# Attention and involution in one kernel: the first block's queries ahead of the last keys, and the last image's products and weights asked for at other points

## The chip, the cores and the metric

The kernel runs on one core of a Trainium2 chip. The metric is the device time of one execution in microseconds (us). Before the change it is 2611.5 us, the median of three runs (2610.78 to 2611.92).

## The reference

The input x is 4 images of 512 channels and 64 x 64 pixels, in float32. Two layers follow each other:

```
# layer 0: attention over all 4096 pixels of an image
q, k, v = wq x + bq, wk x + bk, wv x + bv          # 128 channels each
attn = softmax(q^T k)
x = wo (v attn^T) + bo + x
# layer 1: involution, 7 x 7, in 8 groups of 16 channels
o1 = relu(W1 x * s1 + b1)                          # 128 channels
w  = Ws relu(Wr o1 * sr + br) + bs                 # 49 taps x 8 groups, for every pixel
out[g, c] = sum over taps of w[g, tap] * o1[g, c] shifted by the tap
x = W3 out * s3 + b3 + x
```

## The kernel before, in words

**Tiles and order.** Pixels are cut into 8 chunks of 512 (8 rows of the image). For each image the kernel first makes all keys and values (`keys_values`, line 438), in the order of `KEYS`: chunks 2 to 7, then 1, then 0. For a chunk that is 4 matmuls into `pk`, an activation on ScalarE that writes the keys, 16 matmuls of 128 columns into `pv`, and a copy on ScalarE that writes the values. Then `attention` (line 609) goes through the chunks again as blocks of queries: in each block 32 steps of one score matmul (`pss`), an exp on ScalarE (`pt`), one matmul with the values (`po`) and one add of `pt` on VectorE (`pacc`). Scores are issued two steps ahead of `po`. The queries of a block (`queries`, line 472: 4 matmuls into `pq` and an activation) are made eight steps before the block begins. Only the first block of an image has them made at the head of `attention` (line 617), after the last values. In the last image the last block is split in two halves of 256 pixels (blocks 7 and 8).

**What runs beside attention.** Each finished block is taken over by `finish_block` (line 482), a generator that divides by the softmax sum (`sums`, `blocks`, `pl`, `rls`, `spread`, `on`), projects back (`pwo`), adds the input, makes o1 (`p1`), writes it pixel by pixel to DRAM (`pix`), and makes the reduced channels from which the tap weights follow (`pr`, `red`). The involution (`involution`, line 301) works in units of 4 image rows, 16 in an image. For a unit TensorE makes the tap weights of all its pixels (`weights`, line 270, into the PSUM tile `pw`); VectorE multiplies windows of o1, read back from DRAM into the SBUF tile `ring`, by the weights (`prod`, or `acc` for the first, line 351), 14 to 21 products a unit; and GpSimd adds the products up (line 375). `prod` has 4 buffers. TensorE then turns the sum (`turn_unit`, line 390), and `close_chunk` (line 419) projects it (`py`), adds it to x and stores.

**Who sets the order.** The order is written by the program itself with an account of time. `mm` (line 213) adds each matmul's reckoned time to `pe`, and `takes` adds each operation of another engine to `free[...]`. After every attention step `chores` (line 264) runs one step of the list `finishing`, one of `closing`, and then `pace` (line 227), which offers products as far as they are due and as the account lets VectorE and GpSimd take them (VectorE's queue up to 4.5 us ahead in the last image, 3.5 in the others). A generator that waits for a point of the account uses `until`; in the involution line 308 waits until VectorE will be free, plus 0.3 us, before a unit's weights are made:

```python
            yield from until(free["dve"] + 0.3)
            pw = early.pop((b, u), None) or weights(b, u)
```

A scheduler may then shift instructions that don't depend on each other. While attention runs, `pw` has one PSUM buffer; a second is opened once it is over (line 682).

**The tail.** When the last block's steps are out, `tail` is set. From there nothing waits for the account, every second product is added on TensorE by matmuls with the identity (`pa`) in place of GpSimd, and the rest of `finishing`, `closing` and the units is written out in turns until all is stored.

Of the kernel before, what the change touches and what calls it, by code (L numbers as in the profile page):

```python
# [13 lines left out]
B, C, H, W = 4, 512, 64, 64  # L14
# [3 lines left out]
CH = 512  # L18
# [52 lines left out]
HOP_US = 0.8  # L71
STEP_US = 1.0
POOL_LAG = 4.0, 7.5
PIECE = 3
TB = 32
WARM = 8
# [7 lines left out]
def fast_path(  # L84
# [68 lines left out]
    pe = 0.0  # L153
    due, seen = 0.0, 0.0
    free = {"dve": 0.0, "pool": 0.0, "dma": 0.0}
    tail = []
    reds, sums_c = {}, {}
    written = {}
# [4 lines left out]
    def until(us):  # L163
        while pe < us and not tail:
            yield "wait"
# [9 lines left out]
    def load_x(b, c):  # L175
        xs[b, c] = xpool.tile([P, CT, CH], F32, tag="x", name=f"x_{b}_{c}")
        takes("dma", X_US)
        nc.sync.dma_start(xs[b, c], x_r[b, :, :, c * CH : (c + 1) * CH])
# [38 lines left out]
    def step(queue, n):  # L217
        while n and queue:
            try:
                if next(queue[0]) in ("wait", "none"):  # L220
                    return False
                n -= 1
            except StopIteration:
                queue.pop(0)
        return not n
# [36 lines left out]
                load = (b + 1) * STEP  # L262

    def chores():
        step(finishing, 1)
        step(closing, 1)
        pace()
# [33 lines left out]
    def involution():  # L301
        nonlocal low, due
        while True:
            while not units:
                yield "none"
            b, u = units.pop(0)
            acc = work2.tile([P, NT, 4, P], F32, tag="acc", name=f"acc_{b}_{u}")
            yield from until(free["dve"] + 0.3)
            pw = early.pop((b, u), None) or weights(b, u)
            begin = pe + 0.5  # L310
            pa, ops = None, []
            base = b * STEP + u * UR
            for dy0, n in DYS:

                at = (base + dy0) % RING
                whole = at + n + NT < RING + 1
                pieces = [(dy0, n)] if whole else [(dy0, 2), (dy0 + 2, n - 2)]
                ops += [(x, dy, k) for x in range(K) for dy, k in pieces]
            for o, (x, dy, n) in enumerate(ops):
                if o and dy >= DYS[1][0] > ops[o - 1][1]:  # L320
                    low = base + UR
                    pump()
                    if tail and units:
                        early[units[0]] = weights(*units[0])
                rows = [(base + dy + t * 2) % RING for t in range(NT)]
                while base + dy + n + NT > load:
                    yield "wait"
                landed = max(landing[base + dy + i] for i in range(n + NT))
                while not tail and (
                    pe < max(begin, landed)  # L330
                    or free["dve"] > pe + (4.5 if b == B - 1 else 3.5)
                    or free["pool"] > pe + lag
                ):
                    yield "wait"
                free["pool"] = max(free["pool"], takes("dve", DVE_TAPS[0] + DVE_TAPS[1] * n))
                takes("pool", POOL_TAPS[0] + POOL_TAPS[1] * n)
                due -= n
                d0 = dy - DYS[dy >= DYS[1][0]][0]
                first = x == 0 and dy < DYS[1][0]
                prod, p0 = acc, d0  # L340
                if not first:
                    prod, p0 = prods.tile(
                        [P, NT, 4, P], F32, tag="prod", name=f"prod_{b}_{u}_{o}"
                    ), 0
                col = (x * K + dy) * G
                lines = ring[:, rows[0] : rows[0] + n, x, :]
                image = bass.AP(
                    tensor=lines.tensor, offset=lines.offset,
                    ap=[lines.ap[0], [(rows[1] - rows[0]) * K * P, NT], [K * P, n], [1, P]],
                )  # L350
                product = nc.vector.tensor_tensor(  # L351
                    prod[:, :, p0 : p0 + n, :].rearrange("p t d (g c) -> p t d g c", g=G),
                    image.rearrange("p t d (g c) -> p t d g c", g=G),
                    pw[:, :, col : col + n * G].unsqueeze(3)
                    .broadcast_to([P, NT, n * G, GC])
                    .rearrange("p t (d g) c -> p t d g c", d=n),
                    ALU.mult,
                )
                if lag == POOL_LAG[0]:
                    tc.keep_in_program_order(product)  # L360
                if first:
                    pass
                elif tail and o % 2:

                    begun = pa is not None
                    if not begun:
                        pa = ps1.tile([P, NT, P], F32, tag=("po", "acc")[u % 2], name=f"pa_{b}_{u}")
                    for t in range(NT):
                        for d in range(n):
                            mm(  # L370
                                pa[:, t, :], prod[:, t, d, :], ident,
                                not begun and t == d == 0, False,
                            )
                else:
                    nc.gpsimd.tensor_tensor(  # L375
                        acc[:, :, d0 : d0 + n, :], acc[:, :, d0 : d0 + n, :], prod[:, :, :n, :],
                        ALU.add,
                    )
                yield
            low = max(low, (b + 1) * STEP if u == NU - 1 else base + UR)  # L380
            pump()
            if pa is None:
                for n in (2, 1):
                    nc.gpsimd.tensor_tensor(  # L384
                        acc[:, :, :n, :], acc[:, :, :n, :], acc[:, :, n : 2 * n, :], ALU.add
                    )
            closing.append(turn_unit(b, u, acc, pa, takes("pool", POOL_OP * 1.5)))
# [50 lines left out]
    def keys_values(b):  # L438
        kt = kvpool.tile([P, N], F32, tag="k", name=f"k_{b}")
        vT = kvpool.tile([P, N // P, P], F32, tag="v", name=f"v_{b}")  # L440

        for i, c in enumerate(KEYS):
            for k in KEYS[i + 1 : i + 3]:
                if (b, k) not in xs:
                    load_x(b, k)
            if b < 2 and i == 4:
                for rows in (slice(0, PAD), slice(PAD + H, None)):
                    nc.sync.dma_start(pix[b][rows].rearrange("r w c -> w r c"), zero)
                for cols in (slice(0, PAD), slice(PAD + W, None)):
                    nc.sync.dma_start(pix[b][PAD : PAD + H, cols, :], zero[:H])  # L450
            xt = xs[b, c] if c < KEEP else xs.pop((b, c))
            pk = ps_s.tile([P, CH], F32, tag="s", name=f"pk_{b}_{c}")
            for t in range(CT):
                mm(pk, w_slice(O_WK, t), xt[:, t, :], t == 0, t == CT - 1)
                if t % 2:
                    chores()
            nc.scalar.activation(
                kt[:, c * CH : (c + 1) * CH], pk, AF.Identity, bias=v1(V_BK)
            )
            pv = ps1.tile([P, 4, P], F32, tag=("po", "acc")[i % 2], name=f"pv_{b}_{c}")  # L460
            for j in range(4):
                for t in range(CT):
                    mm(
                        pv[:, j, :], xt[:, t, j * P : (j + 1) * P], w_slice(O_WV, t),
                        t == 0, t == CT - 1,
                    )
                if j % 2:
                    chores()
            nc.scalar.copy(vT[:, 4 * c : 4 * c + 4, :], pv)
        return kt, vT  # L470

    def queries(b, c, off, n):
        xt = xs[b, c][:, :, off : off + n]
# [132 lines left out]
            yield from tell()  # L606


    def attention(b, kt, vT):
        blocks = [(c, 0, CH) for c in range(NCH)]  # L610
        if b == B - 1:

# [1 line left out]

        steps = [(k, j) for k, (_, _, n) in enumerate(blocks) for j in range(N // P * n // CH)]
        qs, pts, pos, paccs = {}, {}, {}, {}
        qs[0] = queries(b, *blocks[0])

        def score(m):
            k, j = steps[m]  # L620
# [47 lines left out]
    for b in range(B):  # L668
        lag = POOL_LAG[0]
        kv = keys_values(b)  # L670
        lag = POOL_LAG[1]
        if b == 0:

            pb = ps.tile([P, CT], F32, tag="mm", name="pb")
            for t in range(CT):
                tc.keep_in_program_order(mm(pb[:, t : t + 1], w_slice(O_WO, t), v1(V_BVC)))
            bo = const.tile([P, CT], F32, name="bo")
            nc.vector.tensor_tensor(bo, pb, vec[:, V_BO : V_BO + CT], ALU.add)
        attention(b, *kv)
    tail.append(True)  # L680
    scorepool.close()
# [405 lines left out]
```

## Time and profile before

| | us |
|---|---|
| median of the runs | 2611.5 |
| profiled execution, its own time | 2612.87 |
| its span, first to last instruction | 2611.1 |
| TensorE busy | 2595.2 |
| VectorE busy | 1864.1 |
| GpSimd busy | 1822.8 |
| ScalarE busy | 854.8 |

The mean granted TensorE clock is 0.998. The 256-column, 512-column and 128-column matmuls in float32 show as two passes each in the trace, so that a count such as x8 stands for four matmuls. In the profile PE is TensorE, PEld its weight loads, DVE VectorE, ACT ScalarE and POOL GpSimd. Nearly all matmuls carry line 215, that of the helper `mm`, and are told apart by their tiles. Times of the timeline count from the start of the span. A wait is shown behind its instruction as the idle time and what ended it.

By stages, from the trace (each stretch in us from the start of the span):

| stretch | length | PE busy | DVE busy | ACT busy | POOL busy |
|---|---|---|---|---|---|
| 0 to 62, first keys and values | 62 | 60.9 | 0.2 | 11.0 | 2.5 |
| 62 to 691 | 629 | 628.2 | 429.7 | 211.8 | 394.4 |
| 691 to 1345 | 654 | 653.2 | 479.3 | 219.1 | 485.2 |
| 1345 to 2000 | 655 | 654.2 | 485.3 | 218.2 | 486.5 |
| 2000 to 2540, last image's attention | 540 | 537.1 | 413.8 | 190.1 | 410.4 |
| 2540 to 2611, the rest | 71 | 61.5 | 55.9 | 4.6 | 43.8 |

### The profile page before, as it was taken

The numbers are of one execution on the slowest core, as the hardware profiler recorded it, in microseconds if no ns is written. First come the engines' busy times: TensorE is split into PE (matmuls) and PEld (weight loads), VectorE is DVE, ScalarE is ACT, GpSimd is POOL, SyncE is SP. The second block draws the span as 40 slices with busy tenths as digits, with TensorE's granted clock in tenths as the row PEclk, the third lists the DMA queues.
The fourth block names the chain that finished last, engine by engine and source line by source line (L and its number), as shares of the span: only waits on it lengthen the run. The fifth ranks groups of instructions, "written<-read, shape, count | busy, mean of one in ns | idle before, by whom it ended". The sixth has DMA issues, their size and how long they took to land.

```text
span 2611.1 us, 24493 instructions
## 1 busy us (share of the span) xinstructions
PE 2595.2 (99%) x7580; PEld 1256.3 (48%) x7580; DVE 1864.1 (71%) x2629; ACT 854.8 (33%) x1426; POOL 1822.8 (70%) x1197
## 2 busy tenths in 40 slices
PE   9999999999999999999999999999999999999998
PEld 7444444445544444444644444444464444444577
DVE  0347887876675787888576677888757668777877
ACT  1333333332233333333223333333323333333330
POOL 0007888878881787888785467888788667777876
PEclk9999999999999999999999999999999999999999
DMA  6033223335514344322641434334462423222343
GB/s 236 1 75 61 71 65 72 75 90 144 153 40 107 61 93 93 88 69 59 166 109 37 103 61 93 93 93 93 92 159 85 107 61 93 68 61 59 75 91 102
DMA packets 143899, 231.71 MB, mean 89 GB/s; under 512 B 57032, under 2 KB 63632, under 8 KB 143632
## 3 DMA queue, kind: packets, MB, share of 16 engines
q1 hardware_dynamic: 143328, 229.71, 36.4%
q8 instruction: 61, 1.00, 0.2%
q14 instruction: 78, 0.64, 0.1%
q10 hardware_dynamic: 432, 0.36, 0.0%
HBM read 187.28 MB, written 42.77 MB: 88 GB/s over the span
## 4 chain that ended last, share of the span: by engine, by line
PE 97%; POOL 1%; DVE 1%; issue 0%; ACT 0%; POOLq 0%; DVEq 0%; ACTq 0%
PE pss L215 34%; PE po L215 33%; PE pv L215 4%; PE pwo L215 4%; PE pk L215 4%; PE pq L215 4%; PE p L215 4%; PE py L215 4%; PE pw L215 2%; POOL acc L375 1%; PE pa L215 1%; PE pr L215 1%; DVE prod L351 1%; PE pa L401 1%; PE pl L215 0%
## 5 line engine op out<-in xcount | busy, mean ns | idle before, releaser
L375 POOL TENSOR_TENSOR acc<-acc,prod 128x768 f32<-128x768 f32 (+3 forms) x1063 | 1700.6, 1618 | 766.4 <-DVE prod L351 711.7
L215 PE MATMUL pss<-q,k 128*128 128x512 f32 (+1 forms) x2112 | 1054.7, 584 | 2.3 <-ACT q L478 2.3
L215 PE MATMUL po<-pt,v 128*128 128x512 f32 (+1 forms) x2112 | 1047.2, 580 | 0.0
L627 ACT ACTIVATE pt<-pss 128x512 f32<-128x512 f32 x1024 | 611.5, 597 | 1225.7 <-PE pss L215 1193.9
L351 DVE TENSOR_TENSOR prod<-ring,pw 128x512 f32<-128x512 f32 (+3 forms) x1092 | 900.6, 849 | 83.3 <-POOL acc L375 81.0
L658 DVE TENSOR_TENSOR pacc<-pacc,pt 128x512 f32<-128x512 f32 x958 | 665.4, 695 | 371.1 <-ACT pt L627 363.2
L215 PEld LDWEIGHTS po<-pt,v 128*128 128x128 f32 x2112 | 398.9, 190 | 480.7 <-issue 460.6
L215 PEld LDWEIGHTS pss<-q,k 128*128 128x128 f32 x2112 | 389.2, 190 | 452.7 <-issue 433.0
L522 DVE SCALAR_TENSOR_TENSOR x<-pwo,bo,x 128x512 f32<-128x512 f32 (+1 forms) x132 | 96.4, 733 | 59.0 <-PE pwo L215 57.5
L215 PE MATMUL py<-accT,wt 128*128 128x512 f32 (+1 forms) x264 | 131.4, 581 | 1.1 <-ACT accT L411 0.5
L215 PE MATMUL pwo<-on,wt 128*128 128x512 f32 (+1 forms) x264 | 130.5, 587 | 0.0
L215 PEld LDWEIGHTS pv<-wt,x 128*128 128x128 f32 x1024 | 119.1, 192 | 15.3 <-issue 15.3
L384 POOL TENSOR_TENSOR acc<-acc 128x512 f32<-128x512 f32 x120 | 119.9, 999 | 9.4
L426 DVE SCALAR_TENSOR_TENSOR x<-py,vec,x 128x512 f32<-128x512 f32 (+1 forms) x132 | 95.8, 726 | 37.3 <-PE py L215 35.7
L215 PE MATMUL pv<-wt,x 128*128 128x128 f32 x1024 | 120.8, 276 | 0.0
L540 ACT ACTIVATE x<-x,vec 128x512 f32<-128x512 f32 (+1 forms) x132 | 92.9, 706 | 82.2 <-PE p L215 77.1
L215 PE MATMUL p<-x,wt 128*128 128x512 f32 (+1 forms) x264 | 119.2, 579 | 0.0
L215 PE MATMUL pk<-x,wt 128*128 128x512 f32 x256 | 117.4, 598 | 0.0
L215 PE MATMUL pq<-x,wt 128*128 128x512 f32 (+1 forms) x264 | 115.5, 580 | 0.0
L351 DVE TENSOR_TENSOR acc<-ring,pw 128x1024 f32<-128x1024 f32 (+1 forms) x84 | 79.4, 963 | 49.4 <-PE pw L215 46.8
L215 PEld LDWEIGHTS pq<-x,wt 128*128 128x128 f32 x264 | 49.8, 190 | 58.7 <-issue 56.4
L215 PEld LDWEIGHTS p<-x,wt 128*128 128x128 f32 x264 | 49.9, 190 | 58.3 <-issue 54.0
(56 smaller groups left out, 734.3 us busy)
## 6 DMA issues: line engine op xcount, KB each, us to landing
x<-x_dram SPq DMA_DIRECT2D x55, 1024.0 KB, 6.1
ring<-pix SPq DMA_DIRECT2D x74, 448.0 KB, 10.8
ring<-pix SPq DMA_DIRECT2D x24, 1344.0 KB, 18.0
out_dram<-x SPq DMA_DIRECT2D x31, 1024.0 KB, 4.4
ring<-pix SPq DMA_DIRECT2D x24, 896.0 KB, 13.9
ring<-pix SPq DMA_DIRECT2D x30, 672.0 KB, 11.1
ring<-pix SPq DMA_DIRECT2D x6, 2240.0 KB, 19.0
pix<-o1t SPq DMA_DIRECT2D x192, 32.0 KB, 1.7
```

Of the source, the lines that this page charges most:

```text
L215: return nc.tensor.matmul(o, lhsT=lhsT, rhs=rhs, start=start, stop=stop)
L351: product = nc.vector.tensor_tensor(prod[:, :, p0 : p0 + n, :].rearrange("p t d (g c) -> p t d g c", g=G), image.rearrange("p t d (g c) -> ...
L375: nc.gpsimd.tensor_tensor(acc[:, :, d0 : d0 + n, :], acc[:, :, d0 : d0 + n, :], prod[:, :, :n, :], ALU.add,)
L384: nc.gpsimd.tensor_tensor(acc[:, :, :n, :], acc[:, :, :n, :], acc[:, :, n : 2 * n, :], ALU.add)
L401: nc.tensor.transpose(pa[:, t, :], acc[:, t, 0, :], ident)
L426: nc.vector.scalar_tensor_tensor(xt[:, t, :], py, v1(V_S3 + t), xt[:, t, :], ALU.mult, ALU.add)
L522: nc.vector.scalar_tensor_tensor(xt[:, t, :], pw, bo[:, t : t + 1], xt[:, t, :], ALU.add, ALU.add)
L540: nc.scalar.activation(xt[:, t, :], xt[:, t, :], AF.Identity, bias=v1(V_B3 + t))
L627: nc.scalar.activation(pt, pss, AF.Exp)
L658: nc.vector.tensor_tensor(paccs[k], paccs[k], pt, ALU.add)
```

## The change

Three things are edited. The first block's queries of each image are made in `keys_values`, ahead of the last chunk's keys, and handed on. In the last image `chores` calls `pace` a second time, ahead of the finishing step. And in the last image a unit's weights are asked for 3.5 us sooner by the account than before.

```diff
+AHEAD_US = 3.5
...
+    ending = []
...
     def chores():
+        if ending:
+            pace()
         step(finishing, 1)
         step(closing, 1)
         pace()
...
-            yield from until(free["dve"] + 0.3)
+            yield from until(free["dve"] + (0.3 if b < B - 1 else 0.3 - AHEAD_US))
             pw = early.pop((b, u), None) or weights(b, u)
...
             for k in KEYS[i + 1 : i + 3]:
                 if (b, k) not in xs:
                     load_x(b, k)
+            if c == 0:
+
+                q = queries(b, 0, 0, CH)
...
-        return kt, vT
+        return kt, vT, q
...
-    def attention(b, kt, vT):
+    def attention(b, kt, vT, q):
...
-        qs[0] = queries(b, *blocks[0])
+        qs[0] = q
...
+        if b == B - 1:
+            ending.append(True)
         attention(b, *kv)
```

## The prediction, made before the result was known

> **What bounds the kernel now.** I read the page first, then TensorE's waits, then single stretches of the timeline. TensorE is busy 99% of the span, and the chain that ended last is almost all TensorE:
>
> ```profile
> PE 2595.2 (99%) x7580; PEld 1256.3 (48%) x7580; DVE 1864.1 (71%) x2629; ACT 854.8 (33%) x1426; POOL 1822.8 (70%) x1197
> ...
> PE 97%; POOL 1%; DVE 1%; issue 0%; ACT 0%; POOLq 0%; DVEq 0%; ACTq 0%
> ```
>
> So only two things can shorten it: idle gaps of TensorE while attention runs, and the tail after the last score, where three engines share the end. The table of windows shows both: 540 us from 2000 hold 537.1 us of TensorE work, the last 71 us only 61.5. TensorE's own waits name the gap between the keys and the first score:
>
> ```profile
> PE pa L215 <- DVE prod L351: 3.5, 3, 2.4
> PE pss L215 <- ACT q L478: 2.3, 3, 0.8
> ```
>
> and the timeline of TensorE (start, length, group, passes, wait) shows its true size, at the second image:
>
> ```profile
> 683.05 3.73 PE L215 MATMUL pv<-wt,x 128*128 128x128 f32 x32
> 686.62 3.60 PE L215 MATMUL pq<-x,wt 128*128 128x512 f32 x8
> 691.00 2.94 PE L215 MATMUL pss<-q,k 128*128 128x512 f32 x6 [0.78 <-ACT q L478]
> 693.77 1.02 PE L215 MATMUL po<-pt,v 128*128 128x512 f32 x2
> ```
>
> A pass of 512 columns takes 0.43 us, eight end their issue at 686.62 + 3.43 = 690.05; the scores start at 691.00. The wait costs 0.95 us.
>
> The tail hangs on the involution. POOL adds a unit's products in 30 us and then idles until the next unit's weights come:
>
> ```profile
> 2513.52 2.07 POOL L384 TENSOR_TENSOR acc<-acc 128x512 f32<-128x512 f32 x2
> 2522.10 20.25 POOL L375 TENSOR_TENSOR acc<-acc,prod 128x1024 f32<-128x1024 f32 x9 [6.51 <-PE pr L215]
> ```
>
> This is unit 12 of the last image. On DVE its products start only when its weights exist, and unit 13, the first that runs wholly in the tail, starts 28 us later:
>
> ```profile
> 2519.60 1.22 DVE L351 TENSOR_TENSOR acc<-ring,pw 128x1024 f32<-128x1024 f32 x1 [2.13 <-PE pw L215]
> ...
> 2530.95 0.68 DVE L661 TENSOR_TENSOR sums<-pacc,pt 128x512 f32<-128x512 f32 x1
> ...
> 2546.81 1.21 DVE L351 TENSOR_TENSOR acc<-ring,pw 128x1024 f32<-128x1024 f32 x1
> ```
>
> Seven products of unit 12 stand after the sums, mixed into the last block's softmax chain. From unit 13 on DVE is the tightest engine: of the 52.6 us from 2546.5 to 2599.1 it is busy 49.0 (TensorE 49.9 by the table, but its matmuls there wait for products; POOL 39.2).
>
> [...] after TensorE stood 2.42 us (waiting at 2536.66) the window 2536 to 2543 has a granted clock of 0.52. [...] a unit's weights wait for the last product of the unit before. No wait of that kind is large in this trace. [...]
>
> **The change, part by part.** Times are on the clock of the profile before.
>
> 1. *Queries before the last keys.* Nothing is added: the same 4 matmuls and one activation, ahead of 4 key and 16 value matmuls (3.43 + 3.57 us), which cover the activation (0.69 us). They read the same x tile as the keys did at that point, and no DMA moves. What is late next: the first score needs keys (activated 3 us earlier), the first po the values, copied in 0.59 us before the first exp can start; the third score waits for that exp as now. So 0.95 us goes in images 1 to 3: **-2.8**. In image 0 the built order had filled the wait with a matmul of block 1 and left 0.16 us: **-0.2**. The last units of the image before, which run beside these blocks, come one step (1.7 us) sooner: the weights of unit 14 had 7.3 us of room, the transposes of 13 and 14 over 8.5: nothing.
>
> 2. *Weights 3.5 us sooner, products on both sides.* I counted matmuls in the two built orders: the weights of units 1 to 12 stand 3.4 to 12.1 us of TensorE work sooner (unit 11 by 7.9, unit 12 by 12.1). Does TensorE then wait for DVE? In the trace the weights come 3.4 to 11 us after the unit before has ended on DVE, since the account overrates DVE. But that unit starts sooner too. Taking each unit's length from the trace (24 to 31 us, POOL's rate) I get rooms of 4 to 12 us, unit 11 and 12: 4.4 and 6. The exception is unit 2: unit 1 waits for rows of the next block, does not end sooner (2147.1), and the weights now stand at 2147.0. I put **+0.4** (0 to 1.5) for it.
>  A product ahead of a finishing step delays that step's DVE work by one product (0.86 to 1.13); behind it would stand a pwo matmul and all scores. The account sees it and moves pwo back one step in the built order, so I cost it at nothing; without that cover 1 us in each of 8 blocks.
>
> 3. *The tail.* With its weights at 2506.5 instead of 2518.6, unit 12 runs its adds in POOL from about 2510 (unit 11 ends there at 2507.5: 6.51 us of idle go), 6 x 2.45 + 6 x 1.89 = 26 us, to 2536. The last product, 12_13, needs the buffer of 12_9, free at 2510 + 14.7 + 3 x 1.89 = 2530.4. The built order has one product of unit 12 behind the sums, not seven, and two odd products more go to POOL (12 fewer matmuls in the tail).
>  Against that, two py matmuls (0.86 each) now stand before attention's end: 2531.8 + 1.7 = 2533.5. From there pl and its latency 0.65, reciprocal 0.12, spread 0.36, the verdict's first step 0.68 (it stands there now), on 0.40: 2535.7, against 2536.8 now. The first pwo at full clock and its drain: x starts 2536.4. Then on TensorE the second pwo, one py (needs the first x's buffer, 2536.9), a third pwo, the second half of unit 13's weights (0.43): 2539.1. Unit 13 starts at about 2539.4 instead of 2546.8: **-7.4**. Rows and weights of units 14 and 15 come from the same chain, 7 us sooner, so nothing there takes its place. Behind it the same products follow at DVE's pace; TensorE has its p1, pp and pr in front of unit 13's first sums and comes about 0.9 us late against now, of which I charge half: **+0.5**.
>
> Sum: -2.8 - 0.2 + 0.4 - 7.4 + 0.5 = **-9.5 us**. The profiled execution took 2612.87 (span 2611.1 and 1.8 around it), 1.4 above the median of the runs, 2611.5; I take the difference to the median: **2602.0**.
>
> Bounds: the tail's DVE idles 3.6 us now; half of it could close (-1.8) and both charges could be nil (-0.9): 2599. The other end is the second rival.
>
> **Rivals.** (a) *The clock halves again.* In the tail TensorE still stands about 1 us before the first pwo. If that starts a half clock of 6.8 us as now, pwo, py and weights on the path (3 us at full clock) take twice as long: -6.5, **2605**. For: it happened at this place. Against: the idle was 2.4 us. (b) *The tail gives it back*: DVE reaches unit 13 sooner but waits there for POOL or for TensorE's sums, or the last store is set by another chain; only the queries count: 2611.5 - 3.0 + 0.4 = **2609**. For: three engines are within 25% of each other there. Against: POOL is done with unit 12 at 2536, 10 us sooner than now. (c) *Weights block TensorE*, slower: if the products of units 1 to 11, now packed denser among the softmax adds, end 7 us later than I reckon, the weights stand 2 us or so before a full buffer in 10 units, and every score behind them waits: +20 - 9.5, **2622**. It decides from rooms of 4 to 6 us on; POOL's 30 us per unit would have to become 36. Nothing in the trace shows that: POOL's longest unit of the last image that does not wait for rows takes 33.
>
> **How the numbers follow.** Chances: forecast 0.72, (a) 0.11, (b) 0.11, (c) 0.06. The range takes the forecast with its bounds and (a) and reaches close to (b): 2599 to 2608. Within 0.2% (5.2 us) no change can be told; forecast and (a) lie beyond it, (b) within: faster 0.83, same 0.12, slower 0.05 (a mild (c) would stay within).
>
> **What would show it.** Right: no wait of pss for q, and pss straight after pv; unit 13's acc on DVE some 10 us sooner (7 after taking off the queries' 3); POOL's gap before unit 12 gone; a mean clock near 1 after 2530. Wrong: TensorE's waits list pw behind DVE products for over 2 us, or pwo or p behind x; DVE idle in the tail well over 3.6 us; the half clock in the same place.

## The result, and the profile after

The changed kernel is slower by half a percent: 2624.34 us, median of five runs (2622.2 to 2625.07), against 2611.5 for the kernel before in the same comparison; the ratio is 1.0049 [1.0038, 1.006]. I had forecast 2602.0 and 2599 to 2608. The profiled execution took 2625.07, its span is 2623.0, 11.9 longer than before.

The first line of the page and TensorE's waits (us in total, times, longest) already hold the answer. This is the page of the kernel after:

```profile
PE 2598.5 (99%) x7556; PEld 1256.2 (48%) x7556; DVE 1871.2 (71%) x2629; ACT 853.7 (33%) x1426; POOL 1825.9 (70%) x1199
```

and these are its waits of TensorE:

```profile
PE py L217 <- DVE rls L515: 11.5, 5, 3.9
PE pl L217 <- DVE blocks L506: 1.6, 1, 1.6
...
PE pl L217 <- DVE x L430: 0.9, 1, 0.9
PE pa L217 <- DVE prod L355: 0.7, 2, 0.4
```

The page says 99% busy as before: TensorE does 24 matmul passes less and still shows 3.3 us more of busy time, because more of it ran at half clock (mean granted clock 0.997, 0.998 before; a pass of 512 columns took 0.85 us there instead of 0.43). The wait of `pss` for `q` is gone, and a new one stands at the top: five `py` matmuls wait 11.5 us for the reciprocal `rls` of a block's softmax sum. Before, there was one such wait of 0.5.

The first edit did what it should. TensorE at the second image (start, length, group, passes):

```profile
678.78 3.60 PE L217 MATMUL pq<-x,wt 128*128 128x512 f32 x8
682.22 3.60 PE L217 MATMUL pk<-x,wt 128*128 128x512 f32 x8
685.65 3.73 PE L217 MATMUL pv<-wt,x 128*128 128x128 f32 x32
689.22 2.84 PE L217 MATMUL pss<-q,k 128*128 128x512 f32 x6
```

The 32 passes of `pv` are followed by `pss` at once. From first score to first score the second and third image take 633.5 us instead of 634.5.

The third edit also did at its own place what I had counted on. GpSimd's idle time of 6.5 us before unit 12 is gone (its 1024-element adds begin straight after the unit before, timeline of POOL after):

```profile
2526.47 2.08 POOL L388 TENSOR_TENSOR acc<-acc 128x512 f32<-128x512 f32 x2
2528.51 16.48 POOL L379 TENSOR_TENSOR acc<-acc,prod 128x1024 f32<-128x1024 f32 x7
```

But all of it happens late. Unit 13 starts at 2558.13, where before it started at 2546.81 (timeline of VectorE after, with the last block's finish in front of it):

```profile
2551.10 0.21 DVE L515 RECIPROCAL rls<-pl 128x8 f32<-128x8 f32 x1
...
2552.84 1.64 DVE L292 SCALAR_TENSOR_TENSOR ok<-rls,ok 128x32 f32<-128x32 f32 x1
...
2554.92 1.08 DVE L529 SCALAR_TENSOR_TENSOR x<-pwo,bo,x 128x256 f32<-128x256 f32 x2 [0.21 <-PE pwo L217]
...
2558.13 1.22 DVE L355 TENSOR_TENSOR acc<-ring,pw 128x1024 f32<-128x1024 f32 x1 [0.36 <-PE pw L217]
```

Cut at the same events, the two profiled executions compare like this (us; negative is a gain):

| stretch | forecast | measured | how measured |
|---|---|---|---|
| queries, four images | -3.0 | -3.2 | 0.16 in image 0, then 0.96, 1.04, 1.04 from first score to first score (one matmul of 0.86, which moves across the first score of image 0, taken off) |
| first loads of the program | none | -0.7 | a `pv` ahead of any edit starts at 22.43, the same one at 23.08 before |
| last image's attention, two `py` more in it | +1.7 | +1.7 | four passes of 0.43 |
| last image's attention, TensorE held up | +0.4 | +19.0 | first score to last `po`: 571.9 before, 592.6 after, less the 1.7 |
| end of attention to unit 13 | -9.1 | -5.6 | 15.0 before, 9.4 after, 5.9 forecast |
| unit 13 to the end | +0.5 | +0.6 | 64.3 before, 64.9 after |
| sum | -9.5 | +11.8 | spans: +11.9 |

So one term carries the whole error. The 19.0 are about 13 us of standing (the waits listed above for `py`, and `pl` once, with the late starts behind them), and about 5 us lost to half clock after such stands (three times 1.7); about 1 us is not accounted for. The windows of the kernel after show the half clock, three times in attention and once in the tail; the columns are the stretch, busy time of PE, PEld, DVE, ACT and POOL, then the granted clock, DMA share and GB/s:

```profile
2250.90:2254.40 3.50, 3.50 (x6) 1.51 (x5) 2.35 (x4) 0.60 (x1) 2.73 (x4) 0.56 0.25 97
```

```profile
2326.10:2329.60 3.50, 3.22 (x4) 1.51 (x5) 2.74 (x6) 0.00 (x0) 3.42 (x2) 0.54 0.00 0
2476.20:2479.80 3.60, 2.98 (x5) 1.77 (x6) 3.60 (x8) 0.00 (x0) 3.48 (x4) 0.55 0.00 0
2551.30:2554.90 3.60, 3.60 (x13) 2.77 (x12) 3.34 (x6) 0.00 (x0) 3.06 (x2) 0.55 0.00 0
```

Each time 3.41 us ran at a granted clock of 0.5. In the first three a pass of 512 columns took 0.85 instead of 0.43, which costs about 1.7 each by my estimate, half of the 3.41. The fourth lies in the tail.

**Why `py` waits for a reciprocal.** The two have no data in common. `pl`, `spread` and `py` are all tiles of one PSUM pool with the tag `mm` and two buffers. `pl` takes one, `spread` the other, and the `py` that follows takes `pl`'s, which is free only when the reciprocal has read it. All five waits of `py` listed above, 11.5 us, end with that reciprocal. So TensorE stands behind VectorE's queue, and the scores behind `py` with it (`pss` at 2250.99 below). At the end of block 3 (TensorE after):

```profile
2244.63 0.40 PE L217 MATMUL pl<-blocks,quads 128*128 128x16 f32 x2 [0.86 <-DVE x L430]
2244.88 1.10 PE L217 MATMUL pss<-q,k 128*128 128x512 f32 x2
2245.82 1.02 PE L217 MATMUL po<-pt,v 128*128 128x512 f32 x2
2250.03 1.12 PE L217 MATMUL py<-accT,wt 128*128 128x512 f32 x2 [3.19 <-DVE rls L515]
2250.99 1.60 PE L217 MATMUL pss<-q,k 128*128 128x512 f32 x2
```

and VectorE at the same place:

```profile
2235.76 0.69 DVE L355 TENSOR_TENSOR prod<-ring,pw 128x512 f32<-128x512 f32 x1 [1.40 <-POOL acc L379]
2238.18 0.42 DVE L355 TENSOR_TENSOR prod<-ring,pw 128x256 f32<-128x256 f32 x1 [1.73 <-POOL acc L379]
...
2241.12 0.68 DVE L668 TENSOR_TENSOR sums<-pacc,pt 128x512 f32<-128x512 f32 x1
...
2247.22 1.00 DVE L355 TENSOR_TENSOR prod<-ring,pw 128x256 f32<-128x256 f32 x2
2248.15 0.74 DVE L430 SCALAR_TENSOR_TENSOR x<-py,vec,x 128x512 f32<-128x512 f32 x1
...
2249.74 0.24 DVE L515 RECIPROCAL rls<-pl 128x16 f32<-128x16 f32 x1
```

`pl` was there at 2245.0, yet its reciprocal ran at 2249.74, behind all that was queued before it. Eight products stand between `sums` and `rls`, six before. The `sums` were late themselves, since the products in front of them had stood for GpSimd, 1.40 and 1.73 us here, until a buffer of `prod` was added up. The same place in the kernel before (timeline of TensorE):

```profile
2247.61 0.29 PE L215 MATMUL pl<-blocks,quads 128*128 128x16 f32 x2
2247.75 1.10 PE L215 MATMUL pss<-q,k 128*128 128x512 f32 x2
2248.69 1.02 PE L215 MATMUL po<-pt,v 128*128 128x512 f32 x2
2250.19 1.13 PE L215 MATMUL py<-accT,wt 128*128 128x512 f32 x2 [0.48 <-DVE rls L508]
```

I count from the start of the exp that the sums need (2235.79 before, 2233.89 after). The reciprocal came 14.1 us later before, 15.9 after. TensorE's own work up to that `py`, waits taken off, was 13.9 before and 12.0 after: its new order brings `py` about one score step nearer. So by this reckoning half of the 3.7 us by which TensorE stood longer there (`pl`'s stand counted) comes from VectorE's lateness (1.8) and half from TensorE's order (1.9).

### The profile page after: what moved, and what is told of

Its sections match the earlier page's. It is cut to its first block, busy times and chain, and to the rows that moved or that the text cites. A ratio compares the mean times of both kernels' runs of the same rounds, so it can differ in the third digit from the quotient of the medians.

```text
span 2623.0 us, 24427 instructions
## 1 busy us (share of the span) xinstructions
PE 2598.5 (99%) x7556; PEld 1256.2 (48%) x7556; DVE 1871.2 (71%) x2629; ACT 853.7 (33%) x1426; POOL 1825.9 (70%) x1199
## 5 line engine op out<-in xcount | busy, mean ns | idle before, releaser
L355 DVE TENSOR_TENSOR prod<-ring,pw 128x512 f32<-128x512 f32 (+3 forms) x1092 | 901.1, 850 | 107.2 <-POOL acc L379 102.3
L217 PE MATMUL py<-accT,wt 128*128 128x512 f32 (+1 forms) x264 | 133.9, 591 | 12.3 <-DVE rls L515 11.5
L217 PEld LDWEIGHTS py<-accT,wt 128*128 128x128 f32 x264 | 49.1, 192 | 69.6 <-issue 47.3
```

Of the source, the lines that this page charges most:

```text
L217: return nc.tensor.matmul(o, lhsT=lhsT, rhs=rhs, start=start, stop=stop)
L355: product = nc.vector.tensor_tensor(prod[:, :, p0 : p0 + n, :].rearrange("p t d (g c) -> p t d g c", g=G), image.rearrange("p t d (g c) -> ...
```

## The experiments

Theory A: the weights asked for sooner move the burst of products onto the end of a block, the reciprocal stands behind it, and `py` behind the reciprocal. A1 says that VectorE gets late because its products stand for buffers that GpSimd still reads; A2 that it is VectorE's own work. Rival B: the second offer of products, ahead of the finishing step, does it. Rival C: VectorE's backlog costs, whatever meets it; `py` only meets it first. All runs are compared with the kernel before on the same chip; its medians there were 2611.71, 2610.96 and 2611.61.

### First set: which of the three edits

`e1_queries_only` is the first edit alone:

```diff
         if ending:
-            pace()
...
-            yield from until(free["dve"] + (0.3 if b < B - 1 else 0.3 - AHEAD_US))
+            yield from until(free["dve"] + 0.3)
```

(In the code the two lines of `if ending` go.)

> The kernel before with the first edit alone: first queries ahead of the last keys. All theories: 3 waits of 0.95 us and one of 0.2 go, 2608 to 2609 (before 2611.5), no wait of pss for q, no new wait of py. If it is slower than before, the moved queries themselves cost something that the trace of the changed kernel doesn't name.

2608.72 us, 0.9989 [0.9982, 0.9996]: the -3.0 of the forecast.

`e2_queries_both_sides` adds the second offer, without the sooner weights:

```diff
-            yield from until(free["dve"] + (0.3 if b < B - 1 else 0.3 - AHEAD_US))
+            yield from until(free["dve"] + 0.3)
```

> Queries, and products offered on both sides of the finishing step; weights asked for as before. Theory A (weights asked for sooner move the burst of products onto the block's end, where the reciprocal stands behind it and py behind the reciprocal): this kernel has none of it, waits of py for rls under 2 us, 2605 to 2609. Rival B (the second offer puts products in front of the reciprocal): waits of py for rls near the 11.5 us of the changed kernel, 2618 to 2624.

2605.78 us, 0.9979 [0.9971, 0.9987]. TensorE waits 0.5 us for `rls`, as before. The second offer doesn't cost; the median is 2.9 lower. Rival B falls. The gain is not work that VectorE had got ahead with: when attention ends it has done 260 products of the last image instead of 258. What goes is the stand of 2.42 us in the tail, and with it the half clock that came after it in the kernel before (6.83 us at 0.5). The four executions of `e1_queries_only` at a granted clock of 1.0 took 2605.5 to 2606.2, as long as this kernel; twelve at 0.998 took 2608.3 to 2609.9.

`e3_queries_sooner` has the sooner weights without the second offer:

```diff
-        if ending:
-            pace()
         step(finishing, 1)
```

> Queries, and weights 3.5 us sooner; products offered on one side as before. Theory A: the waits of py for rls are there (8 us or more), half clock after each of the long ones, 2616 to 2626. Rival B: few of them, 2600 to 2607.

2622.79 us, 1.0044 [1.0027, 1.0061], with nearly the waits of the kernel after (waits of `e3_queries_sooner`):

```profile
PE py L217 <- DVE rls L513: 10.9, 5, 4.5
```

Of the three edits this one makes the loss.

`e4_after_hold_py` keeps the change and lets no closing step (a unit's turn, `py`) run from a block's sums until its `on` is due:

```diff
         step(finishing, 1)
-        step(closing, 1)
+        if not holding:
+            step(closing, 1)
...
+        if late:
+            holding.append(True)
         yield from pause(free["dve"], 3)
         pl = ps.tile([P, CH // TB], F32, tag="mm", name=f"pl_{name}")[:, : n // TB]
...
         yield from pause(takes("dve", DVE_OP * n / CH), 5)
+        if late:
+            holding.clear()
```

> The changed kernel with one thing more: from the sums of a block of the last image until its reciprocal and division are due by the account, closing steps (pa, py) rest; they come after. Theory A: the wait is that of py's PSUM buffer for the reciprocal; py now comes after it, the 11.5 us of waits and the half clock that follows go, 2603 to 2609. Rival C (the backlog of VectorE is what costs, py only meets it first): the next reader of the reciprocal's chain, pwo, waits in py's place, 2615 to 2624.

2614.37 us, 1.001 [1.0003, 1.0017]: 10.0 us of the loss go with the meeting of `py` and `pl`'s buffer. The waits of `e4_after_hold_py` show that not all of it goes:

```profile
PE pwo L217 <- DVE on L525: 3.7, 2, 3.0
...
PE py L217 <- DVE x L534: 1.2, 2, 0.9
...
PE pl L217 <- DVE blocks L507: 1.0, 1, 1.0
PE pwo L217 <- DVE x L534: 1.0, 2, 0.6
```

The longest, 3.0 at 2469.9, stands behind the products in VectorE's queue: take `py` away and `pwo` meets the backlog. Not all are the products' doing, though: the wait of 0.9 for `x` (at 2407.6) and that of 0.6 in the tail have a step of the verdict on the sums (`ok`) in front of them, of 1.69 and 1.65 us. Theory A has the place, rival C is right for a part.

### Second set: what makes VectorE late

`e5_after_prods6` gives the products six buffers in place of four. Its instructions stand in the same order as those of the kernel after on all five engines, so only the waits for buffers differ:

```diff
-    prods = pool("prods", 4)
+    prods = pool("prods", 6)
```

> The changed kernel with 6 buffers for products instead of 4, the order of its work otherwise the same. Theory A1: VectorE is late at the block's end because its products stand for a buffer that GpSimd still reads, and the reciprocal stands behind them. With two more buffers that ends: VectorE's waits for GpSimd fall from 102 us to under 50, py's for rls from 11.5 to under 4, 2606 to 2613. Rival A2: it is VectorE's own work in front of the reciprocal (7 or 8 products, softmax adds): waits of py stay above 8, 2618 to 2625.

2608.56 us, 0.9992 [0.9983, 1.0001]: 15.8 less than the kernel after (14.9 by the two ratios, since the two ran on different chips). VectorE's products stand for GpSimd much less; this is the kernel after,

```profile
DVE prod L355 <- POOL acc L379: 102.3, 149, 2.0
```

and these are the same wait and TensorE's for `rls` in `e5_after_prods6`:

```profile
DVE prod L355 <- POOL acc L379: 33.0, 46, 2.0
...
PE py L217 <- DVE rls L515: 4.6, 2, 2.6
```

How late the sums of a block ran after their last exp had ended (us, blocks 0 to 6 of the last image) shows the same thing on VectorE alone:

| kernel | 0 | 1 | 2 | 3 | 4 | 5 | 6 |
|---|---|---|---|---|---|---|---|
| before | 2.5 | 0.0 | 1.7 | 3.0 | 3.5 | 2.6 | 1.8 |
| after | 2.5 | 0.7 | 3.1 | 6.6 | 5.3 | 3.5 | 4.4 |
| e5_after_prods6 | 2.5 | 0.0 | 0.7 | 4.1 | 1.3 | 1.2 | 0.0 |

At block 3 of `e5_after_prods6` the reciprocal comes 13.7 us after its exp begins, sooner than in the kernel before, and yet `py` waits (its TensorE):

```profile
2246.86 1.13 PE L217 MATMUL py<-accT,wt 128*128 128x512 f32 x2 [2.56 <-DVE rls L515]
```

That is the other half, the order on TensorE: there `py` comes after 11.4 us of TensorE's own work.

`e6_after_quiet_end` offers no products from the last steps of a block until its reciprocal is issued:

```diff
-        if ending:
+        if ending and not quiet:
             pace()
...
-        pace()
+        if not quiet:
+            pace()
...
         nc.vector.reciprocal(rl, pl)
+        quiet.clear()
...
+            if b == B - 1 and j == nj - 2 and k + 1 < len(blocks):
+                quiet.append(True)
```

> The changed kernel, but no products are offered in the last image from two steps before a block's sums until its reciprocal is issued; what was held comes after. If products in front of the reciprocal are the cause, by A1 or A2: py's waits for rls under 2 us, no half clock while attention runs, 2602 to 2610. If TensorE waits as long as before at other places (weights for a full buffer, pwo): 2615 to 2624.

2612.72 us, 1.0008 [0.9999, 1.0016]. It takes off 11.6, less than the buffers did. Waits are left: `py` for `rls` 4.1 in three, `pwo` for `on` 2.0, and the mean granted clock is 0.998. The edit didn't do all that it was meant to do. In the built order between none and five products still stand between a block's sums and its reciprocal (two to eight in the kernel after), five of them in front of the longest wait, 2.2 us at 2467.9; and the sums are no less late than in the kernel after (7.9 us at block 3, 6.6 there), since the products asked for earlier still stand in front of them. `pwo`'s longest wait, 1.6 us in the tail, stands behind a step of the verdict of 1.48 us and not behind a product. So this run doesn't tell how much the products in front of the reciprocal cost by themselves.

`e7_ahead_half` asks for the weights 1.75 us sooner, not 3.5:

```diff
-AHEAD_US = 3.5
+AHEAD_US = 1.75
```

> The changed kernel with 1.75 us in place of 3.5. If the cost grows with how early the weights come: 2611 to 2618, between the 2605.8 of no earlier weights and the 2624.3 of 3.5. If any earlier weights bring the burst onto the block's end: 2619 to 2625.

2615.63 us, 1.0017 [1.001, 1.0024]. With `e2_queries_both_sides` (nothing sooner, 2605.8) and the kernel after (2624.3) it makes nearly a line: 5 to 6 us for each us asked sooner. Half the time costs about half as much; amounts under 1.75 us weren't tried.

`e8_sooner_unit12_only` asks sooner only where I had forecast the gain, from unit 12 on:

```diff
-            yield from until(free["dve"] + (0.3 if b < B - 1 else 0.3 - AHEAD_US))
+            yield from until(free["dve"] + (0.3 if (b, u) < (B - 1, 12) else 0.3 - AHEAD_US))
```

> Queries, products on both sides, and the weights 3.5 us sooner for unit 12 alone, the last one before the tail: no block's end with a reciprocal that other work waits for follows it but the last. Theory A: none of the waits, less of unit 12 left for the tail than without (2605.8): 2602 to 2606. If sooner weights cost by themselves: 2608 or more.

2606.88 us, 0.9985 [0.9978, 0.9991]; `e2_queries_both_sides`, without it, had 2605.78. Nothing is won, even at the place and without the loss elsewhere. Unit 13 does start sooner, at 2536.3 instead of 2537.8 (by 0.9 us when counted from the image's first score), but then takes VectorE 22.9 us instead of 19.9. The forecast's rival (b), the tail gives it back, is what happens.

### Third set: what is left when the stands are gone

`e9_both_sides_prods6` is the second offer with six buffers, the weights as before; `e10_before_prods6` is the kernel before with six buffers (a control: what the buffers are worth by themselves); `e11_hold_prods6` is the whole change with six buffers and the hold of `e4_after_hold_py`. In each, next to what is shown above:

```diff
-    prods = pool("prods", 4)
+    prods = pool("prods", 6)
```

> Queries, products on both sides, weights as before, and 6 product buffers. The control for the runs with 6 buffers that is also the best candidate: the version with 4 (2605.8) has no waits of TensorE that come from products, so by A1 two more buffers change only the tail: 2603 to 2606. If the two buffers gain 10 us or more here too, they gain by something else than the waits of py, and the run with 6 buffers says nothing of the change.

> The kernel before with 6 product buffers, nothing else: control. By A1 within 3 us of the kernel before, 2608 to 2613, as TensorE waits for nothing there that stands behind a product, but for the 2.4 us in the tail.

> The changed kernel with 6 buffers and with closing steps resting from a block's sums until the division is due. If the backlog in front of the reciprocal and py's place behind it are the whole of the loss: no wait of py for rls, none of pwo over 1 us, no half clock in attention, 2600 to 2606. If a wait for pwo stays as with 4 buffers (3.7 us): 2608 to 2612.

| kernel | us | ratio to before | `prod` stands for GpSimd | TensorE waits for `rls` or `on` |
|---|---|---|---|---|
| e9_both_sides_prods6 | 2602.69 | 0.9966 [0.9954, 0.9979] | 24.0 | none |
| e10_before_prods6 | 2608.99 | 0.9992 [0.9983, 1.0] | 26.1 | none |
| e11_hold_prods6 | 2605.99 | 0.9979 [0.9972, 0.9987] | 33.7 | 1.3 |

The buffers alone are worth 2.6 to 3.1 us (`e10_before_prods6`; and `e9_both_sides_prods6` against `e2_queries_both_sides`; in both the scheduler also moved some instructions on VectorE), but about 15 under the sooner weights. The difference, 12 to 13 of the 19 us, is what GpSimd's hold on the product buffers did: A1. The profiled executions show it at its place: six buffers shorten the last image's attention by 14.4 us under the sooner weights, and by 0.8 in the kernel before.

The whole change with six buffers and the hold (2606.0) is still 3.3 us slower than the same without the sooner weights and the hold (2602.7). Most of that is standing again: TensorE still stands 2.9 us in its attention (1.3 for `on` as in the table, 1.6 of `py` for `x`), and not at all in `e9_both_sides_prods6`; and the tail gains next to nothing beyond the one `py` that moved ahead of it.

`e9_both_sides_prods6` is the fastest version found. TensorE's waits in it list no softmax step at all; the longest after the program's start is that for GpSimd in the tail, which the kernel before has too:

```profile
PE pa L217 <- POOL acc L379: 1.4, 1, 1.4
...
PE pa L217 <- DVE prod L355: 0.4, 1, 0.4
PE pwo L217 <- DVE x L430: 0.3, 1, 0.3
```

## Why the prediction was wrong

**Part 1, the queries, held.** Forecast -3.0, measured -3.2 in the profile and -3.0 by `e1_queries_only`.

**Part 2 failed, at two sentences.** The first: "A product ahead of a finishing step delays that step's DVE work by one product ... The account sees it and moves pwo back one step in the built order, so I cost it at nothing; without that cover 1 us in each of 8 blocks." The cover was the account's word, and I took it for the chip's. What I missed is a third thing behind a finishing step besides `pwo` and the scores: a `py`, which shares two PSUM buffers with `pl` and `spread`. And the delay is not one product of 0.9 us. It is a run of products that GpSimd holds up: at block 3 the sums come 6.6 us late, 3.0 before. `e2_queries_both_sides` shows that the offer which I had in mind there costs nothing; `e3_queries_sooner` shows that the sooner weights do it. That route, from the third edit through VectorE's backlog to a `py` at the block's end, was not in my sum at all. Size: 19.0 us for a term that I had at +0.4.

The second: "Taking each unit's length from the trace (24 to 31 us, POOL's rate) I get rooms of 4 to 12 us". A length measured with the old start isn't a property of the unit. Those that need the next block's rows start sooner and then wait for them, so they get longer (unit 3 pauses 14.7 us in its middle, 5.9 before): unit 7 took VectorE 41.0 us instead of 30.7, unit 3 33.7 instead of 24.3, unit 5 32.6 instead of 24.3. I had seen this for unit 2 only. The rooms that I had at 4 to 12 shrank to 0.05 to 2 us in front of units 2, 4, 6, 8, 10 and 12. The weights themselves hardly waited for it (0.1 us at most). But on VectorE two units now followed each other after 2 to 3 us at these places, where 4 to 11 had been, and the pause had moved into the middle of a unit. My reading is that the old pauses had let VectorE catch up before a block's end; what is measured is that its products stood 102.3 us for GpSimd, 81.0 before.

**Part 3, the tail.** From attention's end to unit 13 I had 5.9 us, it took 9.4. The `pl` of the last half block waited 1.60 us for `blocks`, behind products; the verdict's second step took 1.64 us instead of 0.18; and the half clock came again, 3.41 us from 2551.7. The last is rival (a), and its place was right. The +0.5 behind unit 13 was +0.6.

**The rivals.** (c), weights block TensorE, at 0.06, had the sign, the size (2622) and the words "every score behind them waits"; its buffer was wrong. I reckoned it for the buffer of the weights alone and found room there. I argued against it from POOL's longest unit that doesn't wait for rows, 33 us against a needed 36; what grew were the units that do wait for rows (unit 7 to 41.0 us on VectorE). (b) is shown by `e8_sooner_unit12_only`, as far as that run goes: without the loss in attention the sooner weights gain nothing.

**What stays open.** Six buffers leave 4.6 us of `py` waiting in `e5_after_prods6`; how much of that is the order on TensorE and how much the eight products was reckoned at one block and not tried alone; `e11_hold_prods6`, which moves that `py` away, is 2.6 us faster. More than six product buffers, and a PSUM buffer of its own for `pl`, weren't tried. The reason of the slow verdict step wasn't looked for; it was as slow in `e5_after_prods6` (1.65), and took 0.18 in `e3_queries_sooner` with the same instruction (`on`) in front of it.

## What to carry to other kernels

Before you move a burst of work on an engine that has slack on average, list everything on the bound engine that waits for an instruction behind that burst, and include the waits by buffer: who shares a rotating buffer with whom, and who must have read it. Count the burst at the pace of its slowest consumer (here GpSimd, through four product buffers: its adds of 1024 elements took 2360 ns on average in the kernel before, VectorE's products of that size 1211), not at its own. And a step's measured length holds only as long as its start and its inputs keep their distance.

## What the runs showed of the hardware that I had not expected

The granted clock was halved after some stands of TensorE and not after others, and the length of a stand alone doesn't tell which. Ahead of the last stores the trace of the kernel after has four stretches at a granted clock of 0.5, of 3.41 us each, from 2251.3, 2326.4, 2476.6 and 2551.7; the kernel before has one, of 6.83 us from 2535.9. These are the stands of TensorE of 0.7 us or more in the two executions, but for that of 1.06 us at the program's start:

| kernel | stand from | us | half clock after it |
|---|---|---|---|
| before, first score of images 1 to 3 | 690.2, 1324.8, 1959.3 | 0.78 each | none |
| before, tail | 2534.2 | 2.42 | 6.83 us from 2535.9 |
| before, tail | 2583.6 | 1.39 | none |
| after, attention | 2172.3 | 0.84 | none |
| after, attention | 2243.8 | 0.86 | none |
| after, attention | 2246.8 | 3.19 | 3.41 us from 2251.3 |
| after, attention | 2323.8 | 2.58 | 3.41 us from 2326.4 |
| after, attention | 2403.7 | 1.00 | none |
| after, attention | 2472.9 | 3.91 | 3.41 us from 2476.6 |
| after, tail | 2548.9 | 1.60 | 3.41 us from 2551.7 |
| after, tail | 2595.3 | 1.38 | none |

The same stand had both outcomes. The kernel before stood 2.42 us in the tail, and ran at half clock from 2535.9 on (windows of the kernel before):

```profile
2535.70:2542.50 6.80, 5.84 (x19) 5.16 (x20) 4.31 (x7) 0.00 (x0) 6.41 (x4) 0.52 0.00 0
```

In `e1_queries_only` the same matmul stood as long (its TensorE, and its windows), and the clock stayed full:

```profile
2532.55 0.68 PE L217 MATMUL pa<-ident,prod 128*128 128x128 f32 x4 [2.42 <-DVE prod L353]
```

```profile
2532.70:2539.60 6.90, 6.90 (x42) 5.99 (x42) 6.59 (x12) 1.75 (x4) 6.67 (x4) 1.00 0.00 0
```

In attention it was so too: the stand of 2.58 us at 2323.8 of the kernel after was followed by half clock, and that of 2.56 us which `e5_after_prods6` had ahead of the `py` at 2246.86 was not. The two passes of that `py` took 1.13 us, those of the `py` at 2326.38 in the kernel after 2.08, and the mean granted clock of the profiled `e5_after_prods6` is 1.0. What decides between the two outcomes, these runs don't show.

For a forecast it means that a stand in attention of the lengths seen here, 2.56 to 3.91 us, can cost about 1.7 us on top by the estimate above, and doesn't always, and that single executions of one kernel can differ by that: 55 executions of the kernel before took 2608.6 to 2613.0 us, the 17 at a granted clock of 1.0 no more than 2609.8.
